# A four-layer graph network on one core: the Mamba block with chunks of 2, 2, 3, 4, 4, 4, 4, 3 tiles, the convolution in six paced steps per tile, taps and statistics one step later

## The chip, the core and the metric

The kernel runs on one core of a Trainium2 chip. It is one program, written in Python on the Tile framework, which traces the operations in program order, gives them priorities, orders them per engine and sets the semaphores. The engines are TensorE (PE: matmuls; its weight loads are PEld), VectorE (DVE), ScalarE (ACT), GpSimd (POOL) and SyncE (SP, which issues the DMAs). The metric is the device time of one execution in microseconds (us).

## What is computed

Four layers of a graph network on n = 3327 nodes with 256 features, all in float32. After each layer x becomes layernorm(x + layer(x, adj)). The change touches layer 1 alone, which is a graph convolution followed by a Mamba block:

```python
h = relu(adj @ x @ gcn_w + gcn_b)
h = layernorm(h) * ln_g + ln_b
xz = h @ w_in;  xc, z = xz[:, :512], xz[:, 512:]
u = silu(sum(xpad[k:k + L] * conv_w[:, k] for k in range(4)) + conv_b)
dbc = u @ w_xp
dt = softplus(dbc[:, :16] @ w_dt + b_dt)
B, C = dbc[:, 16:32], dbc[:, 32:]
dA = exp(dt[:, :, None] * -exp(A_log)[None])
h_t = dA_t * h_(t-1) + dt_t * B_t * u_t        # one scan along the nodes, for each of 512 channels x 16 states
y = (h_t @ C_t + u * D_skip) * silu(z)
out = y @ w_out
```

Layer 0 (a mean over neighbours), layer 2 (graph attention) and layer 3 (two steps of diffusion with a nucleus search) stand before and behind it. Layer 2 needs, for each row tile of layer 1's result, its product with a weight matrix and two attention columns; the program calls these the values and computes them in layer 1's stage.

## The kernel before

The 3327 nodes are 26 tiles of 128 rows (the last padded). In layer 1 three pieces of work run beside each other.

**The convolution** (`convolve`, lines 264 to 330) is a generator over the 26 tiles. For a tile it loads a column block of the adjacency matrix in three DMAs (line 275, 9 + 9 + 8 tiles of 128x128, `JC = 9`, two buffers), and sums 26 products into one PSUM bank `cb` (L276; each float32 matmul is two PE instructions in the profile). Then come a copy (L282), two transposes (L290), a copy (L292), the product with `gcn_w` (L294), the bias (L295) and relu (L297). What is left of the tile is put into a list `rest` that the next tile's loop works off: `measure` (bn_stats on VectorE, L84, then a power on GpSimd, L261, L262, L306), an empty step, `norm` (L309) and `turn` (transposes L318, two scaled copies into `hT`, L320). The generator yields four times for a tile: after j = 8 and 17, after the copy, and at the end. A tile counts as finished when it is turned, which is while the next tile is convolved; only the first tile does all its `rest` at once.

**The scan** goes through chunks of consecutive tiles, at most four (`WC = 512` columns). The chunks have 1, 2, 3, 4, 4, 4, 4, 4 tiles. For each chunk and each of 16 states, a "state" below, the main loop issues: two row loads from a DRAM scratch (L461), four scans on VectorE (L257, one for each group of 128 channels), their decays dA on ScalarE into two PSUM banks (L253), a copy of the last column (L566), the product with C (L257, 128x2048 at four tiles), the multiplication of dt u with B two states ahead on GpSimd (`feed`, L476), and transposes of the product that are summed in PSUM (`add_up`, L497, a bank for each tile of the chunk).

**The next chunk's inputs** are made by a generator `head(c + 1)`, one step in each of states 3 to 14 (lines 373 to 436): four projections (L369), each copied (L383) and multiplied by the first tap on ScalarE (L384), while VectorE adds three more taps to the group of the step before (L257, `u`); silu; `w_sp` (L398); the copy L401 and two DMAs to the scratch; two steps with two `w_dt` products each (L415, L417, L418); a step of exponentials and sums (L422, L423); then the logarithm and three operations of VectorE for `dt`; then `du` and the D-skip. Before state 3's step the main loop runs the convolution until all tiles of chunk c + 1 are finished. Beside that, each state of the main loop ends with one convolution step (`pump`, in the first chunk three of four states), and, when the convolution has ended, with one call of `values` instead (transposes L355, copy L357, product L360, two attention columns and an exponential L361 to L364). In states 0 to 5 gates (L502), residuals (L508, L510, L518, L519) and gate inputs (L445) of the old and the new chunk are added.

What orders this: each engine works off its queue in order. VectorE's scans, products, taps and dt operations are tied into one chain in program order (`chained`), ScalarE's decays and big activations into another (`decaying`); all else the framework places. One PSUM bank, `ps`, is shared by the projections, `w_sp`, `w_dt`, the turn, the gate inputs, the residuals and the values; each must be read out by ScalarE or VectorE before TensorE may write the next one.

The lines in which the pace is set:

```python
                ends.append(min(npad, prev + min(WC, (len(ends) + 1) * P)))
...
            pump(tiles=ends[0] // P)
            xs = {}
            for i, x in enumerate(head(0)):
                if i % 2:
                    pump()
...
                if DS - 13 <= s < DS - 1 and c + 1 < nch:
                    if s == DS - 13:
                        pump(steps=0, tiles=ends[c + 1] // P)
                        ahead = head(c + 1)
                    xs[c + 1] = next(ahead)
...
                if c or s % 4 < 3:
                    pump()
```

Of the kernel before, what the change touches and what calls it, by code (L numbers as in the profile page):

```python
# [9 lines left out]
F32 = mybir.dt.float32  # L10
BF16 = mybir.dt.bfloat16
I32 = mybir.dt.int32
AF = mybir.ActivationFunctionType
# [5 lines left out]
P = 128  # L19
# [3 lines left out]
J0 = 4  # L23
JC = 9
WC = 512
DI = 512
NG = DI // P
# [16 lines left out]
def gnn_kernel(ctx: ExitStack, tc: tile.TileContext, n: int, a: dict, out: bass.AP):  # L44
# [109 lines left out]
    with tc.tile_pool(name="l1b", bufs=1) as wpool, tc.tile_pool(name="l1at", bufs=2) as l1at:  # L154
# [33 lines left out]
        with tc.tile_pool(name="l1aw", bufs=1) as cwork, tc.tile_pool(name="l1c", bufs=2) as ch, \  # L188
# [54 lines left out]
            while not ends or ends[-1] < npad:  # L243
                prev = ends[-1] if ends else 0
                ends.append(min(npad, prev + min(WC, (len(ends) + 1) * P)))
            nch = len(ends)
# [17 lines left out]
            def convolve():  # L264
# [3 lines left out]
                for it in range(nt):  # L268
                    cb = cpsum.tile([P, 2, D], F32, name="cb")
                    acc, tp = cb[:, 0, :], cb[:, 1, :]  # L270
                    for j in range(nt):
                        if j % JC == 0:
                            m = min(JC, nt - j)
                            at = l1at.tile([P, JC, P], F32, name="at")
                            nc.sync.dma_start(at[:, :m, :], a["adjT"][it][:, j:j + m, :])
                        nc.tensor.matmul(acc, at[:, j % JC, :], X0[:, j, :], start=(j == 0), stop=(j == nt - 1))  # L276
                        if j % JC == JC - 1:
                            if rest:
                                rest.pop(0)()
                            yield full  # L280
                    m = cwork.tile([P, D], F32, name="m")
                    nc.scalar.copy(m, acc)  # L282
                    if rest:
                        rest.pop(0)()
                    yield full
                    if rest:
                        rest.pop(0)()
                        full += 1
                    for k in range(2):
# [21 lines left out]
                    def turn(it=it, h=h):  # L311
# [20 lines left out]
            stream = convolve()  # L332
            done = 0
            ready, valued = 0, 0

            def pump(steps=1, tiles=0):


                nonlocal done
                while steps > 0 or done < min(tiles, nt):  # L340
                    t = next(stream, None)
                    if t is None:
                        return values()
                    done, steps = t, steps - 1

            def values():

                nonlocal valued
                if valued == ready:
                    return  # L350
                it = valued
                valued += 1
# [11 lines left out]
                nc.scalar.mul(F[:, it, :D], po[:, :D], g)  # L364

            def project(c, g, w):
# [6 lines left out]
            def head(c):  # L373
# [6 lines left out]
                u = us[c] = ch.tile([P, NG, WC], F32, name="u", bufs=1)[:, :, :w]  # L380
                for g in range(NG + 1):
                    if g < NG:
                        nc.scalar.copy(xc[:, g, 3:3 + w], project(c, g, w))  # L383
                        nc.scalar.activation(u[:, g, :], xc[:, g, 0:w], AF.Identity, scale=conv_w[:, g, 0:1],  # L384
                                             bias=conv_b[:, g:g + 1])
                    if g:
                        ug = u[:, g - 1, :]
                        for k in range(1, 4):
                            chained(nc.vector.scalar_tensor_tensor, ug, xc[:, g - 1, k:k + w], conv_w[:, g - 1, k:k + 1], ug,
                                    op0=ALU.mult, op1=ALU.add)  # L390
                    if g < NG:
                        yield None
# [36 lines left out]
                dt = ch.tile([P, NG, WC], F32, name="dt", bufs=2)[:, :, :w]  # L429
                chained(nc.vector.scalar_tensor_tensor, dt, v, 0.0, e1, op0=ALU.max, op1=ALU.add)  # L430
                du = ch.tile([P, NG, WC], F32, name="du", bufs=1)[:, :, :w]
                yield None
                chained(nc.vector.tensor_mul, du, dt, u)
# [121 lines left out]
            for k, (c, s) in enumerate(states):  # L555
# [13 lines left out]
                if DS - 13 <= s < DS - 1 and c + 1 < nch:  # L569
                    if s == DS - 13:  # L570
                        pump(steps=0, tiles=ends[c + 1] // P)
                        ahead = head(c + 1)
                    xs[c + 1] = next(ahead)
# [32 lines left out]
            while valued < nt:  # L606
                values()


# [805 lines left out]
```

## Time and profile before

| | us |
|---|---|
| runs: median of three | 3623.58 |
| runs: lowest, highest | 3621.65, 3624.86 |
| the profiled execution | 3620.64 |
| its span, first to last instruction | 3618.6 |
| layer 1's stage in it: from layer 0's last aggregation matmul to layer 2's first | 354.0 to 1504.3 |
| first scan, last scan's end | 398.5, 1456.9 |

The span is 2.0 us shorter than the execution's own time, and that execution is 2.9 us faster than the median of the runs. In the page, "busy" is the time in which an engine had an instruction in work. In a window's row each engine has its busy time with the number of instructions in brackets, then the granted clock of TensorE as a share of full speed, the DMA share and the rate. A list of waits says which instruction stood idle for which other one, with the total, the number of times and the longest. In a timeline the columns are the start, the duration, the engine, the line, the operation, out<-in, shapes, how many were merged, and in brackets the idle time before it with what ended it. Lines of the Mamba block's chained operations are those of the helpers (L257 for VectorE, L253 for ScalarE); their tiles tell them apart: `h` is a scan, `hc` the product, `u` a tap, `dA` a decay, `t` and `dt` the softplus.

### The profile page before, as it was taken

How to read it: one execution, taken by the hardware profiler on the slowest of the kernel's cores; microseconds unless marked ns; L12 is line 12 of the kernel's file. 1: busy time of each engine (PE TensorE's matmuls, PEld its weight loads, DVE VectorE, ACT ScalarE, POOL GpSimd, SP SyncE). 2: the span in 40 equal slices, each digit the busy share in tenths (PEclk: the TensorE clock that was granted, in tenths of full speed). 3: DMA queues.
4: the chain of work that ended last, by engine and by line, in shares of the span. 5: the costliest groups of instructions: out<-in, count | busy, mean ns of one | idle time of the engine just before them, and what ended most of it. 6: DMA issues, size and time to landing. Idle time of an engine off the chain costs nothing. (4 is left out here: it accounts for less than half of the span.)

```text
span 3618.6 us, 43460 instructions
## 1 busy us (share of the span) xinstructions
PE 3287.3 (91%) x15583; PEld 2564.1 (71%) x15583; DVE 2414.3 (67%) x5460; ACT 1707.9 (47%) x2642; POOL 939.9 (26%) x970
## 2 busy tenths in 40 slices
PE   9999888888888765799979999999999899999996
PEld 7888666666666444588858777787786667777775
DVE  1111377889899888577753545445451999999996
ACT  1000465656656555211133333333335888888883
POOL 0000144556566545111110000000000233333332
PEclk9999999989998878799989999999999999999998
DMA  7443334334333122244422122121122122222210
GB/s 247 136 138 99 105 99 105 109 91 121 95 99 95 54 54 64 82 139 150 145 63 65 52 59 63 47 66 52 58 63 65 48 61 63 68 68 68 68 57 22
DMA packets 151997, 308.03 MB, mean 85 GB/s; under 512 B 19858, under 2 KB 73266, under 8 KB 151634
## 3 DMA queue, kind: packets, MB, share of 16 engines
q1 hardware_dynamic: 151762, 305.06, 28.1%
q8 instruction: 127, 2.08, 0.2%
q14 instruction: 108, 0.88, 0.1%
HBM read 294.36 MB, written 10.65 MB: 84 GB/s over the span
## 5 line engine op out<-in xcount | busy, mean ns | idle before, releaser
L476 POOL TENSOR_TENSOR h<-du,row 128x2048 f32<-128x2048 f32 (+3 forms) x128 | 475.3, 3714 | 432.9 <-DVE hc L257 301.9
L257 DVE TENSOR_TENSOR_SCAN h<-dA,carry,h 128x512 f32<-128x512 f32 (+2 forms) x448 | 496.8, 1153 | 47.2 <-ACT dA L253 46.9
L253 ACT ACTIVATE dA<-dt,A_log 128x512 f32<-128x512 f32 (+3 forms) x512 | 308.0, 609 | 241.4 <-DVE h L257 240.2
L858 PE MATMUL acc<-F,at 128*128 128x256 f32 x1352 | 352.5, 386 | 1.0 <-ACT q L632 0.6
L891 PE MATMUL acc<-X,wt 128*128 128x256 f32 x1352 | 343.6, 390 | 10.5 <-ACT wt L889 10.2
L891 PE MATMUL acc<-G,wt 128*128 128x256 f32 x1352 | 336.3, 392 | 5.9 <-ACT wt L822 5.3
L497 PE MATMUL y<-ident,hc 128*128 128x128 f32 x1664 | 256.3, 309 | 76.8 <-DVE hc L257 76.5
L276 PE MATMUL cb<-F,at 128*128 128x256 f32 x1352 | 320.9, 387 | 5.3 <-ACT hn L297 3.2
L497 PEld LDWEIGHTS y<-ident,hc 128*128 128x128 f32 x1664 | 224.5, 161 | 133.1 <-DVE hc L257 100.1
L891 PEld LDWEIGHTS acc<-X,wt 128*128 128x128 f32 x1352 | 242.5, 189 | 105.3 <-issue 41.3
L116 PE MATMUL acc<-xa,at 128*128 128x257 f32 x1352 | 309.1, 382 | 5.7 <-DMA at<-in_adjT 5.7
L858 PE MATMUL acc<-X,at 128*128 128x256 f32 x1352 | 308.4, 381 | 0.0
L767 PE MATMUL acc<-F,at 128*128 128x257 f32 x1352 | 303.9, 381 | 0.9 <-DMA U<-in_U 0.9
L276 PEld LDWEIGHTS cb<-F,at 128*128 128x128 f32 x1352 | 254.8, 194 | 59.1 <-issue 17.6
L891 PEld LDWEIGHTS acc<-G,wt 128*128 128x128 f32 x1352 | 250.1, 193 | 65.7 <-ACT wt L822 35.6
L903 DVE MAX8 cand<-e 128x8 f32<-128x128 f32 x676 | 142.3, 280 | 228.6 <-ACT e L844 217.1
L858 PEld LDWEIGHTS acc<-F,at 128*128 128x128 f32 x1352 | 237.1, 190 | 75.1 <-issue 50.2
L116 PEld LDWEIGHTS acc<-xa,at 128*128 128x128 f32 x1352 | 256.0, 191 | 42.7 <-issue 5.6
L858 PEld LDWEIGHTS acc<-X,at 128*128 128x128 f32 x1352 | 252.9, 191 | 39.8 <-issue 7.8
L767 PEld LDWEIGHTS acc<-F,at 128*128 128x128 f32 x1352 | 253.6, 191 | 36.6 <-issue 1.1
L257 DVE TENSOR_TENSOR hc<-h,row 128x2048 f32<-128x2048 f32 (+3 forms) x128 | 245.4, 1917 | 5.7 <-PE y L497 0.5
L889 ACT COPY wt<-tp 128x512 f32<-128x512 f32 (+1 forms) x182 | 93.7, 557 | 309.5 <-PE tp L887 308.9
(302 smaller groups left out, 5180.3 us busy)
## 6 DMA issues: line engine op xcount, KB each, us to landing
at<-in_adjT SPq DMA_DIRECT2D x102, 832.0 KB, 4.5
at<-in_adjT SPq DMA_DIRECT2D x260, 320.0 KB, 3.0
row<-bc SPq DMA_DIRECT2D x80, 512.0 KB, 4.8
at<-in_adjT SPq DMA_DIRECT2D x52, 576.0 KB, 4.3
at<-in_adjT SPq DMA_DIRECT2D x26, 512.0 KB, 3.8
row<-bc SPq DMA_DIRECT2D x16, 384.0 KB, 5.0
row<-bc SPq DMA_DIRECT2D x16, 256.0 KB, 4.8
xt<-in_xT SPq DMA_DIRECT2D x26, 128.0 KB, 4.1
```

The source lines that it names most:

```text
L116: nc.tensor.matmul(acc, at[:, j, :], rhs[:, j0 + j, :], start=(j0 + j == 0), stop=(j0 + j == nt - 1))
L253: decays.append(nc.scalar.activation(*x, **k))
L257: chain.append(op(*x, **k))
L276: nc.tensor.matmul(acc, at[:, j % JC, :], X0[:, j, :], start=(j == 0), stop=(j == nt - 1))
L476: nc.gpsimd.tensor_tensor(hs[k % 2][:, :, :w], du, rows[k][:, 0:1, :].to_broadcast([P, NG, w]), op=ALU.mult)
L497: nc.tensor.matmul(y[:, g * P:(g + 1) * P], h[:, g, i * P:(i + 1) * P], ident, is_transpose=True, start=(first and g == 0), stop=(last and ...
L767: nc.tensor.matmul(acc, at[:, j, :], F[:, j0 + j, :], start=(j0 + j == 0), stop=(j0 + j == nt - 1))
L858: nc.tensor.matmul(acc, at[:, j, :], rhs[:, j0 + j, :], start=(j0 + j == 0), stop=(j0 + j == nt - 1))
L889: copy(wt[:, :m, :], pt[:, :m, :])
L891: nc.tensor.matmul(acc, wt[:, j, :], rhs[:, j0 + j, :], start=(j0 + j == 0), stop=(j0 + j == nt - 1))
L903: nc.vector.max(cand[:, s * 8:(s + 1) * 8], z[:, s * SEG:(s + 1) * SEG])
```

## The change

The chunks become 2, 2, 3, 4, 4, 4, 4, 3 tiles. The convolution yields six times for a tile (after j = 5, 11, 17, 23, after the copy with all that is left of `rest`, and at the end), and `rest` begins with an empty step, so that the statistics come one step later. Instead of one step for each state, `pace` runs as many steps as keep the convolution even over the states, so that the tiles of chunk c + 1 are finished when state 3 of chunk c comes; in chunk 0's head it runs too. When the convolution has ended, `pace` makes two half values for each state: `value` yields between the copy of the transposed tile and the product. In `head` VectorE adds the taps of the group of two steps before, which takes one more step; the two `w_dt` steps issue their exponentials themselves, the second is issued in one step with the sums, and the early issue of the `w_dt` products is gone. The silu of the gate is issued in state 8 instead of 7.

```diff
-                ends.append(min(npad, prev + min(WC, (len(ends) + 1) * P)))
+                ends.append(min(npad, prev + min(WC, max(2, len(ends) + 1) * P)))
...
-                        if j % JC == JC - 1:
+                        if j % JM == JM - 1 and j < nt - 1:
                             if rest:
                                 rest.pop(0)()
                             yield full
                     m = cwork.tile([P, D], F32, name="m")
                     nc.scalar.copy(m, acc)
-                    if rest:
-                        rest.pop(0)()
+                    while rest:
+                        step = rest.pop(0)
+                        step()
+                        full += step is turn
                     yield full
-                    if rest:
-                        rest.pop(0)()
-                        full += 1
...
-                    rest = [measure, lambda: None, norm, turn]
+                    rest = [lambda: None, measure, lambda: None, norm, turn]
...
+            def advance():
+                nonlocal done, taken
+                t = next(stream, None)
+                if t is not None:
+                    done, taken = t, taken + 1
+                return t is not None
+
+            def pump(tiles):
+                while done < min(tiles, nt) and advance():
+                    pass
+
+            def pace(c, s):
+                c, s = divmod(c * DS + s + DS - 3, DS)
+                t0 = ends[c] if c < nch else npad
+                t1 = ends[c + 1] if c + 1 < nch else npad + P
+                target = NS * (t0 + (t1 - t0) * (s + 1) / DS) / P + NS - 1
+                while taken < target:
+                    if not advance():
+                        for _ in range(2):
+                            values()
+                        return
...
                 xt = cwork.tile([P, D], F32, name="m")
                 nc.scalar.copy(xt, pt[:, :D])
+                yield
                 po = psum.tile([P, WC], F32, name="ps")
...
+            def values():
+                nonlocal valued, valuing
+                if next(valuing, valuing) is None:
+                    return
+                if valued < ready:
+                    valuing = value(valued)
+                    valued += 1
+                    next(valuing)
...
-                for g in range(NG + 1):
+                for g in range(NG + 2):
...
-                    if g:
-                        ug = u[:, g - 1, :]
+                    if g > 1:
+                        ug = u[:, g - 2, :]
...
                 for g0 in range(0, NG, 2):
-                    pair = [psum.tile([P, WC], F32, name="ps") for _ in range(2)]
-
-                    with tc.high_priority():
-                        for g, ps in enumerate(pair, g0):
-                            k = slice(32 * g, 32 * g + DTR)
-                            nc.tensor.matmul(ps[:, :w], w_dt[k, :P], left[k], start=True, stop=True)
-                    for g, ps in enumerate(pair, g0):
+                    for g in range(g0, g0 + 2):
+                        ps = psum.tile([P, WC], F32, name="ps")
+                        k = slice(32 * g, 32 * g + DTR)
+                        nc.tensor.matmul(ps[:, :w], w_dt[k, :P], left[k], start=True, stop=True)
                         nc.scalar.activation(v[:, g, :], ps[:, :w], AF.Identity, bias=b_dt[:, g:g + 1])
                         nc.scalar.activation(e[:, g, :], ps[:, :w], AF.Abs, bias=b_dt[:, g:g + 1])
-                    yield None
+                        nc.scalar.activation(e[:, g, :], e[:, g, :], AF.Exp, scale=-1.0)
+                    if not g0:
+                        yield None
                 e1 = scratch()[:, :, :w]
                 for g in range(NG):
-                    nc.scalar.activation(e[:, g, :], e[:, g, :], AF.Exp, scale=-1.0)
                     nc.scalar.activation(e1[:, g, :], e[:, g, :], AF.Identity, bias=1.0)
...
-            pump(tiles=ends[0] // P)
+            pump(ends[0] // P)
             xs = {}
             for i, x in enumerate(head(0)):
-                if i % 2:
-                    pump()
+                pace(0, 3 - DS + i)
...
-                if s == 7:
+                if s == 8:
                     decaying(szs[c], szs[c], AF.Silu)
...
-                if c or s % 4 < 3:
-                    pump()
+                pace(c, s)
```

`JM` and `NS` are 6. `DS` is 16 states, `P` 128 rows, `nt` 26 tiles, `nch` 8 chunks.

More of the change, by code (lines that the diff above doesn't have):

```diff
@@ L24 @@
 JC = 9
+JM = 6
+NS = 6
 WC = 512
@@ L332, in gnn_kernel, with value @@
             stream = convolve()
[L333 to L352, printed above, removed]
+            done = taken = 0
+            ready, valued, valuing = 0, 0, iter(())
+            def advance():
[17 more added lines that the diff above has]
+                        return
+            def value(it):
                 pt = psum.tile([P, WC], F32, name="ps")
@@ L364, in values @@
                 nc.scalar.mul(F[:, it, :D], po[:, :D], g)
+                yield
+            def values():
[6 more added lines that the diff above has]
+                    next(valuing)
             def project(c, g, w):
@@ L385, in head @@
                                              bias=conv_b[:, g:g + 1])
-                    if g:
-                        ug = u[:, g - 1, :]
+                    if g > 1:
+                        ug = u[:, g - 2, :]
                         for k in range(1, 4):
-                            chained(nc.vector.scalar_tensor_tensor, ug, xc[:, g - 1, k:k + w], conv_w[:, g - 1, k:k + 1], ug,
-                                    op0=ALU.mult, op1=ALU.add)
-                    if g < NG:
+                            chained(nc.vector.scalar_tensor_tensor, ug, xc[:, g - 2, k:k + w], conv_w[:, g - 2, k:k + 1],
+                                    ug, op0=ALU.mult, op1=ALU.add)
+                    if g < NG + 1:
                         yield None
@@ L430, in head @@
                 chained(nc.vector.scalar_tensor_tensor, dt, v, 0.0, e1, op0=ALU.max, op1=ALU.add)
+                yield None
                 du = ch.tile([P, NG, WC], F32, name="du", bufs=1)[:, :, :w]
-                yield None
                 chained(nc.vector.tensor_mul, du, dt, u)
@@ L566, in gnn_kernel @@
                     nc.scalar.copy(carry[:, s, :], hs[k % 2][:, :, w - 1])
-                if s == 7:
+                if s == 8:
                     decaying(szs[c], szs[c], AF.Silu)
-                if DS - 13 <= s < DS - 1 and c + 1 < nch:
-                    if s == DS - 13:
-                        pump(steps=0, tiles=ends[c + 1] // P)
+                if 3 <= s < DS - 1 and c + 1 < nch:
+                    if s == 3:
+                        pump(ends[c + 1] // P)
                         ahead = head(c + 1)
@@ L607, in gnn_kernel @@
                 values()
+            values()
     half = nt // 2 * P
```

## The prediction

> **What bounds the kernel now.** The page's first and second parts came first: the change lies in one stage, the Mamba block, and the shares of the whole span say little about it.
>
> ```profile
> span 3618.6 us, 43460 instructions
> ...
> PE 3287.3 (91%) x15583; PEld 2564.1 (71%) x15583; DVE 2414.3 (67%) x5460; ACT 1707.9 (47%) x2642; POOL 939.9 (26%) x970
> ```
>
> The page's chain that ended last names only the final store, so the stage was cut by hand into windows at the first scan of each chunk (found in the timeline: 398.5, 487.3, 589.0, 722.6, 874.5, 1023.5, 1172.0, 1330.3, last scan done 1456.9). First row: start-up before any scan; then the eight chunks of 1, 2, 3, 4, 4, 4, 4, 4 tiles; last row: the tail up to layer 2.
>
> ```profile
> core 0: us, PE busy (x) PEld busy (x) DVE busy (x) ACT busy (x) POOL busy (x), PEclk, DMA share, GB/s
> 354.00:398.00 44.00, 40.57 (x193) 31.85 (x192) 10.37 (x28) 19.82 (x47) 3.93 (x9) 1.00 0.29 92
> 398.00:487.00 89.00, 77.05 (x334) 57.76 (x334) 48.27 (x104) 51.67 (x143) 27.57 (x30) 0.92 0.35 100
> 487.00:589.00 102.00, 92.01 (x430) 68.83 (x429) 80.36 (x109) 65.14 (x145) 46.41 (x34) 0.95 0.43 112
> 589.00:722.00 133.00, 115.55 (x516) 84.29 (x515) 108.60 (x114) 77.88 (x147) 66.66 (x37) 0.90 0.39 102
> 722.00:874.00 152.00, 133.27 (x635) 100.01 (x633) 136.17 (x117) 86.89 (x150) 87.76 (x34) 0.92 0.37 107
> 874.00:1023.00 149.00, 127.65 (x616) 95.67 (x616) 136.77 (x121) 87.96 (x152) 88.67 (x35) 0.93 0.36 104
> 1023.00:1172.00 149.00, 118.72 (x576) 88.80 (x576) 137.46 (x121) 87.85 (x152) 89.13 (x35) 0.91 0.31 89
> 1172.00:1330.00 158.00, 110.12 (x448) 72.96 (x448) 135.18 (x113) 93.63 (x183) 76.88 (x23) 0.78 0.21 54
> 1330.00:1457.00 127.00, 78.77 (x390) 61.04 (x390) 115.79 (x97) 64.16 (x129) 71.44 (x19) 0.83 0.22 58
> 1457.00:1504.00 47.00, 32.78 (x117) 23.02 (x117) 14.52 (x42) 13.58 (x35) 4.22 (x12) 0.67 0.14 54
> ```
>
> The third busy column is DVE. In the eight chunks it sums to 898.6 us of 1059, so VectorE with its scans is the bound, with 160.4 us idle: 40.7, 21.6, 24.4, 15.8, 12.2, 11.5, 22.8, 11.2 by chunk. TensorE is busy 87 to 90% in chunks 1 to 3, so there it is nearly the bound too. The start-up holds 10 us of DVE work in 44. Next, what DVE waited for in this stage (354 to 1504):
>
> ```profile
> engine line waited for: us in total, times, longest us
> DVE h L257 <- ACT dA L253: 59.5, 50, 5.7
> DVE bnst L84 <- ACT hn L297: 57.8, 11, 17.3
> DVE u L257 <- ACT u L384: 51.8, 27, 5.2
> DVE X L519 <- PE ps L518: 16.6, 4, 7.2
> ```
>
> The second line is statistics of a convolved tile standing in DVE's queue ahead of scans, the third the convolution taps doing so: both block scans behind them until ScalarE delivers. The fourth is the tail.
>
> **1. Start-up.** With a first chunk of two tiles the program waits for two finished tiles, and a tile is finished (turned) only in the next tile's last part, so three tiles are convolved before the first projection, where one was. Rows of the timeline:
>
> ```profile
> 367.74 0.44 PE L290 MATMUL cb<-ident,m 128*128 128x128 f32 x2 [0.51 <-ACT m L282]
> ...
> 370.92 2.00 PE L276 MATMUL cb<-F,at 128*128 128x256 f32 x8 [0.47 <-ACT hn L297]
> ...
> 375.15 0.61 PE L369 MATMUL ps<-hT,w_in 128*128 128x128 f32 x4
> ...
> 417.81 11.41 PE L276 MATMUL cb<-F,at 128*128 128x256 f32 x52
> ```
>
> A dense convolution is 11.4 us, its tail (from 367.2 to the next tile's start at 370.9) 3.7. So: 370.9 + 11.4 + 0.4 (the turn) + 3.7 + 11.4 = 397.9; the turn of tile 1 and its two ScalarE copies (0.4 + 0.4 + 2 x 0.4, as at 373.6 to 375.15) put the first projection at about 400, 25 later than 375.15. The head of chunk 0 then took 23.4 us (375.15 to 398.5) at one tile. At two tiles, in the built program's order, 24 pairs of convolution matmuls (0.44 us each) lie between its first projection and w_sp where 13 did (+4.8), four projections take 1.03 instead of about 0.65 (+1.5), and a gcn and bias piece of 1.8 with half a us of waiting for its accumulator stands among them: +9. The w_dt part: +2 (ScalarE rows of 256 instead of 128 columns). The DVE chain of four (0.69 each at one tile, half of the 2.3 at four tiles, 1.15, at two), and the first feed, 2.35 for 1.27: +3. First scan at about 437.5, **+39 us**. A second count agrees: before the first product's transposes TensorE now has 5.0 tiles of convolution where it had 2.7, 2.3 x 15.1 = 35 us. Bounds 30 and 46.
>
> **2. DVE work.** The tiles are the same 26 and the instructions as many; only widths move. Scans (rows 409, 734, 999, 1267 ns for 1 to 4 tiles): 2 x 0.734 + 2 x 0.999 + 4 x 1.267 against 0.409 + 0.734 + 0.999 + 5 x 1.267, times 64: +3.6. Products (831, 1304, 1755, 2289 ns, times 16): -1.0; taps (351, 565, 619, 752, times 12): +1.0. **+3.6 us.**
>
> **3. Idle time in the chunks.** Chunk 0 of one tile goes: its 40.7 idle us were the forced convolution (19.0 for statistics, one wait of 17.3; 12.6 for dA). Taps come a step later: the data they read were issued a whole state earlier, so their 46.6 us inside chunks (51.8 less 5.2 in the start-up) should go; what is late next is dA, whose waits I keep. Statistics come a sixth of a tile later: their waits shrink to 0 to 2. Merging the second w_dt pair with the exponentials puts 6 x 0.65 + 4 x 0.62 + the state's 4 x 0.69 = 9.1 us on ScalarE in one state of 7.1 DVE us; the old layout had up to 7.8. ScalarE is 57 to 59% busy in the four-tile windows and the scheduler spreads it, so 0, with 2 a chunk if that cover fails. TensorE, counted from the built order at full clock, gets 62, 86, 103, 108 and 112 us in chunks 0 to 4, where the old order had 83, 100, 115 and 113 in chunks 1 to 4: so c1 and c2 stay near TensorE's bound and I leave 5 us each for it. Convolution still ends in chunk 5, so the last two chunks hold the same value work, in two steps: the tap waits of c6 go (5.5), its 6.4 for e1 and 10.0 for dA stay; c7 has ten values instead of nine beside states of 5.3 us instead of 7.1, I take 12. Idle by chunk after: c0 11 (21.6 of the old two-tile chunk, less 7.9 for taps and 2.8 of its 4.8 for statistics), c1 16 (that and 5), c2 16 (24.4 - 9.4 - 4 + 5), c3 10 (15.8 - 8.2 + 2 for TensorE), c4 6 (12.2 - 6.2), c5 6 (11.5 - 5.1), c6 17, c7 12, in all 94: **-66 us**. Bounds: 60 (dA waits shrink too) and 141 (every width idles as now: 21.6 + 21.6 + 24.4 + 15.8 + 12.2 + 11.5 + 22.8 + 11.2).
>
> **4. Tail.** Three last tiles instead of four, three values instead of four. The timeline gives residuals 3.8 to 5.6 apart (1462.4, 1466.2; 1482.6 to 1488.2) and 4.2 per value (1488.7 to 1492.9): **-9 us**; bounds -6 and -12.
>
> **At nothing.** The adjacency loads keep size and number (78), and so do the row loads; on SP's queue a row load may stand behind an adjacency load that waits for its buffer, but all matmuls waited 2.1 us for such loads in this stage, and POOL's multiplications have 2.6 us of slack per four-tile state (7.1 less 4.5). The table loads are as many in both built programs. The D-skip and du edits move an allocation, no instruction. If POOL's cover failed it would be 1 us in some states.
>
> [...] The granted clock was 0.90 to 0.95 in the chunks with convolution and 0.78 and 0.83 in the last two without. [...] By the rows it is 0.9 still, since total work per chunk stays. I take the rows.
>
> **Sum.** 39 + 3.6 - 66 - 9 = -32 us. The profiled execution took 3620.6 (span 3618.6 and 2 around it): 3588. The median of the runs is 2.9 above that execution: **3591**.
>
> **Rivals.**
> (a) The waits change their name: taps no longer wait for u, but scans behind them wait for dA or the product's transposes as long. For it: ScalarE's queue is in order, dA is already the largest wait (59.5), and c1 to c3 have TensorE near 90%. Against it: the tap waits are short (1 to 2 us) and sit in states whose dA came in time. Then idle is 141 and the sum 39 + 3.6 - 19 - 9 = +14, **3638, slower**. The point that decides: idle in the chunks above 127 us.
> (b) TensorE takes over in c1 to c4 only: 7 more us each than forecast: 3591 + 28, **3619**, within 0.2%.
> (c) The dA waits shrink as well, since fewer bunches stand ahead of them, and the start-up comes at its lower bound: idle 60, first scan +31: 39 - 8 + 3.6 - 100 - 9 = -74, **3549**.
> (d) The scheduler undoes the pacing: its built order was read, and taps and statistics do stand a state later, so this is only a small chance, and falls under (b).
>
> **Chances and range.** Forecast 0.60 (3570 to 3608), (a) 0.14, (b) and (d) 0.14, (c) 0.12. The range leaves out most of (a) and half of (c): 3560 to 3622. A measurement here can tell about 0.2% from no change, 7 us. Faster by more than that: the forecast, (c) and a third of (b), 0.77; within: most of (b) and an edge of (a), 0.11; slower: 0.12.
>
> **What would show it.** Right: first scan at 432 to 443; no wait of u on ACT u in the chunks above 1 us; idle between 85 and 105; four-tile chunks of 141 to 146 us before convolution ends; tail near 38. Wrong: first scan beyond 446, or dA waits above 80 us in the stage, or a granted clock near 0.8 in chunks 1 to 5.

## The result, and the profile after

The changed kernel takes 3631.39 us (median of 20 runs, 3622.35 to 3638.18) against 3621.19 before (20 runs): the ratio is 1.0025, 95% interval 1.0017 to 1.0034. It is a quarter of a per cent slower, where 3591 us, about 0.9% faster, was forecast.

The page of the profiled execution (3631.3 us):

```profile
span 3629.5 us, 43459 instructions
...
PE 3275.3 (90%) x15583; PEld 2562.6 (71%) x15583; DVE 2412.7 (66%) x5460; ACT 1709.0 (47%) x2642; POOL 937.9 (26%) x967
```

The same work in 11 us more. The windows, cut again at the first scan of each chunk; first row the start-up, last row the tail:

```profile
core 0: us, PE busy (x) PEld busy (x) DVE busy (x) ACT busy (x) POOL busy (x), PEclk, DMA share, GB/s
354.00:442.00 88.00, 82.33 (x333) 64.70 (x332) 15.07 (x31) 28.77 (x60) 7.92 (x15) 0.90 0.32 95
442.00:526.00 84.00, 69.86 (x332) 52.98 (x331) 72.08 (x102) 57.85 (x136) 44.30 (x26) 0.92 0.38 100
526.00:630.00 104.00, 92.30 (x448) 70.72 (x446) 80.50 (x111) 66.24 (x146) 48.23 (x34) 0.97 0.42 110
630.00:766.00 136.00, 115.86 (x539) 85.32 (x538) 111.00 (x114) 78.34 (x147) 68.40 (x35) 0.94 0.38 103
766.00:918.00 152.00, 126.03 (x592) 91.93 (x592) 134.71 (x116) 86.83 (x150) 86.20 (x34) 0.91 0.35 101
918.00:1075.00 157.00, 126.51 (x616) 95.29 (x616) 136.87 (x122) 88.35 (x152) 86.48 (x34) 0.91 0.35 98
1075.00:1224.00 149.00, 107.10 (x522) 79.55 (x522) 136.62 (x122) 85.96 (x146) 86.76 (x34) 0.89 0.29 80
1224.00:1371.00 147.00, 99.47 (x448) 70.87 (x448) 131.17 (x113) 89.70 (x183) 76.13 (x21) 0.84 0.22 56
1371.00:1471.00 100.00, 67.02 (x328) 51.40 (x328) 90.32 (x95) 56.42 (x131) 54.27 (x19) 0.84 0.28 56
1471.00:1510.00 39.00, 25.00 (x95) 18.00 (x95) 12.72 (x39) 11.06 (x29) 3.20 (x9) 0.70 0.17 62
```

The start-up holds 88 us instead of 44, as meant. The tail is 39 instead of 47. The second chunk has two tiles as before and lasts 104 us where it took 102, with the same 80.5 us of VectorE. The four-tile chunk at 918 takes 157 us where the one at 874 took 149, with the same 136.9 us of VectorE (136.8 before). What VectorE waited for in the stage (354 to 1510):

```profile
engine line waited for: us in total, times, longest us
DVE bnst L86 <- ACT hn L298: 64.3, 9, 16.5
DVE h L259 <- ACT dA L255: 55.9, 43, 4.2
DVE t L259 <- ACT t L445: 46.6, 7, 12.4
DVE u L259 <- ACT u L408: 23.8, 6, 16.1
```

The taps (`u`) fell from 51.8 to 23.8, and of these 20.7 lie in the start-up: inside the chunks they wait 3.1 us instead of 46.6, as forecast. But `t`, the first operation of the softplus, now stands third with 46.6 us of waiting for the sums on ScalarE. Before, the same table had it far down:

```profile
DVE t L257 <- ACT t L423: 7.0, 2, 6.4
```

Inside the chunks the taps lost 43.5 us of waiting and t gained 33.4 (6.4 to 39.8): most of the time that left one line came back under another.

How it comes about, in the four-tile chunk at 918. First the kernel before, the timeline of the w_dt series that makes t:

```profile
965.76 1.12 PE L415 MATMUL ps<-t,w_dt 16*128 16x512 f32 x2 [0.21 <-ACT t L401]
...
987.18 0.63 ACT L423 ACTIVATE t<-t 128x512 f32<-128x512 f32 x1
...
990.20 2.27 DVE L257 SCALAR_TENSOR_TENSOR t<-t 128x2048 f32<-128x2048 f32 x1
```

From the first product to the last sum are 22 us, about three states of 7.1; VectorE comes to t at 990.2, 2.4 us after the series has ended, and does not wait. The same series in the changed kernel:

```profile
1019.73 1.12 PE L437 MATMUL ps<-t,w_dt 16*128 16x512 f32 x2
...
1025.72 0.69 ACT L255 ACTIVATE dA<-dt,A_log 128x512 f32<-128x512 f32 x1 [2.73 <-DVE h L259]
1026.34 0.67 ACT L438 ACTIVATE t<-ps,b_dt 128x512 f32<-128x512 f32 x1
...
1027.64 2.07 PE L437 MATMUL ps<-t,w_dt 16*128 16x512 f32 x2 [5.01 <-ACT t L439]
...
1032.47 0.63 PE L319 MATMUL ps<-ident,hn 128*128 128x128 f32 x2
...
1034.37 1.12 PE L437 MATMUL ps<-t,w_dt 16*128 16x512 f32 x2
...
1036.85 1.12 PE L437 MATMUL ps<-t,w_dt 16*128 16x512 f32 x2 [0.88 <-ACT t L439]
...
1040.20 1.66 ACT L445 ACTIVATE t<-t 128x512 f32<-128x512 f32 x3
...
1041.89 2.29 DVE L259 SCALAR_TENSOR_TENSOR t<-t 128x2048 f32<-128x2048 f32 x1 [12.41 <-ACT t L445]
...
1046.52 4.53 POOL L498 TENSOR_TENSOR h<-du,row 128x2048 f32<-128x2048 f32 x1 [17.40 <-DVE hc L259]
```

Each product writes the one bank `ps`, and the next may start only when ScalarE has read it twice; ScalarE's queue has the decays ahead of that reading (the one at 1025.72 itself waited 2.73 us for a scan), and a turn (L319) takes the bank in between. From 1019.7 to 1041.9 are again 22 us. ScalarE is not the limit by its load: in the window 1019 to 1042 it is busy 15.8 of 23 us. But t now stands in VectorE's queue 9.8 us after the first product, so it waits 12.4, and the product, the scans and GpSimd (17.4 us idle) stand behind it.

Measured so in every trace (**series**: first w_dt product's start to the last sum's end; **room**: that start to the moment VectorE comes to t), for the heads that prepare chunks 3 to 6 (four tiles in both kernels):

| kernel | series, us | room, us |
|---|---|---|
| before | 16.3, 21.7, 22.0, 21.7 | 19.2, 24.1, 24.4, 24.1 |
| changed | 18.8, 17.6, 22.1, 17.5 | 15.3, 7.6, 9.8, 19.8 |

The series is about as long as before; what the change took away is the room. In the head for chunk 3 even 10.6 of the 15.3 us are a wait: the statistics of a convolved tile stand in VectorE's queue just ahead of t.

### The profile page after: what moved, and what is told of

Same layout as the page of the kernel before. It is cut to its first block, busy times and chain, and to the rows that moved or that the text cites. A ratio compares the mean times of both kernels' runs of the same rounds, so it can differ in the third digit from the quotient of the medians.

```text
span 3629.5 us, 43459 instructions
## 1 busy us (share of the span) xinstructions
PE 3275.3 (90%) x15583; PEld 2562.6 (71%) x15583; DVE 2412.7 (66%) x5460; ACT 1709.0 (47%) x2642; POOL 937.9 (26%) x967
## 3 DMA queue, kind: packets, MB, share of 16 engines
HBM read 294.36 MB, written 10.65 MB: 84 GB/s over the span
## 5 line engine op out<-in xcount | busy, mean ns | idle before, releaser
L498 POOL TENSOR_TENSOR h<-du,row 128x2048 f32<-128x2048 f32 (+2 forms) x128 | 475.6, 3716 | 411.4 <-DVE hc L259 310.3
L259 DVE TENSOR_TENSOR_SCAN h<-dA,carry,h 128x512 f32<-128x512 f32 (+2 forms) x448 | 478.8, 1113 | 54.3 <-ACT dA L255 51.3
L255 ACT ACTIVATE dA<-dt,A_log 128x512 f32<-128x512 f32 (+2 forms) x512 | 309.0, 609 | 232.0 <-DVE h L259 228.0
L912 PE MATMUL acc<-X,wt 128*128 128x256 f32 x1352 | 345.2, 392 | 10.5 <-ACT wt L910 10.2
L278 PE MATMUL cb<-F,at 128*128 128x256 f32 x1352 | 333.6, 397 | 12.2 <-ACT hn L298 12.1
L278 PEld LDWEIGHTS cb<-F,at 128*128 128x128 f32 x1352 | 263.6, 200 | 69.2 <-ACT hn L298 18.2
L519 PEld LDWEIGHTS y<-ident,hc 128*128 128x128 f32 x1664 | 217.2, 157 | 130.9 <-DVE hc L259 100.0
L879 PEld LDWEIGHTS acc<-X,at 128*128 128x128 f32 x1352 | 252.9, 191 | 39.8 <-issue 6.6
L259 DVE TENSOR_TENSOR hc<-h,row 128x2048 f32<-128x2048 f32 (+2 forms) x128 | 246.5, 1926 | 4.7
```

What stands on the lines that cost most here:

```text
L255: decays.append(nc.scalar.activation(*x, **k))
L259: chain.append(op(*x, **k))
L498: nc.gpsimd.tensor_tensor(hs[k % 2][:, :, :w], du, rows[k][:, 0:1, :].to_broadcast([P, NG, w]), op=ALU.mult)
L519: nc.tensor.matmul(y[:, g * P:(g + 1) * P], h[:, g, i * P:(i + 1) * P], ident, is_transpose=True, start=(first and g == 0), stop=(last and ...
L879: nc.tensor.matmul(acc, at[:, j, :], rhs[:, j0 + j, :], start=(j0 + j == 0), stop=(j0 + j == nt - 1))
L912: nc.tensor.matmul(acc, wt[:, j, :], rhs[:, j0 + j, :], start=(j0 + j == 0), stop=(j0 + j == nt - 1))
```

## The experiments

Theory: the merged step gives t too little room, and this wait cancels what the later taps save. Rivals: the pacing, the chunks or the dropped early issue cost the time. The kernel before was run beside each set and came to 3620.5 to 3621.4 us, so the medians can be compared across sets. Ratios to before have intervals of about 0.0009 to 0.0013 on either side, 3 to 5 us. Each trace is one execution and can lie some us from its run's median: e5's took 3603.2 us, e10's 3589.2, e16's 3602.7.

**e1 and e2: the head step alone, undone or done.** e1 is the changed kernel with before's `head`; e2 is before with the changed `head`. The edit, to and fro:

```diff
-                    if g > 1:
-                        ug = u[:, g - 2, :]
+                    if g:
+                        ug = u[:, g - 1, :]
...
+                    pair = [psum.tile([P, WC], F32, name="ps") for _ in range(2)]
+                    with tc.high_priority():
...
-                        nc.scalar.activation(e[:, g, :], e[:, g, :], AF.Exp, scale=-1.0)
-                    if not g0:
-                        yield None
+                    yield None
                 e1 = scratch()[:, :, :w]
                 for g in range(NG):
+                    nc.scalar.activation(e[:, g, :], e[:, g, :], AF.Exp, scale=-1.0)
```

> The changed kernel with the whole head step of before (w_dt products in two steps and issued early, exponentials in a third, taps one group after their projection); chunks, pacing and values stay changed. Theory (the merged w_dt and exponential step makes a new wait that cancels what the taps saved): the wait of DVE's t for ScalarE falls from 46.6 us to under 12, the taps' wait for u inside the chunks returns from 3.1 us to 25 to 47, and the time stays within 0.3% of the changed kernel, 3622 to 3641 us. Rival 1 (the head's edits are a gain of some 40 us that the pacing or the chunks eat): 3660 us or more. Rival 2 (the head's edits are a pure loss): 3605 us or less.

Measured: 3624.46 us, ratio 1.0008 (0.9999 to 1.0017). t's wait is 7.0, the taps' is 42.6 inside the chunks.

> The kernel before with the changed head step alone. Theory (the merged step makes its wait wherever it stands): taps' waits for u inside the chunks fall from 46.6 us to under 5, the wait of t for ScalarE rises from 7.0 to 35 to 50, and the time is within 0.3% of before, 3610 to 3632 us. Rival (the wait at t needs the new pacing, which puts a turn and a convolution tail beside it): t waits under 15 us and the time is 3580 to 3595 us.

Measured: 3618.44 us, ratio 0.9993 (0.9984 to 1.0003). The waits inside its chunks (399 to 1450):

```profile
DVE t L257 <- ACT t L421: 44.6, 7, 9.4
...
DVE u L257 <- ACT u L384: 8.9, 4, 4.8
```

Both times and t's wait are as the theory has it (the taps in e2 keep 8.9 us, not under 5): the head's edits exchange one wait of some 45 us for another, with the old pacing too. They are worth -3 us in the old kernel, which is within its interval, and +7 in the new.

**e3 and e4: the chunks alone**, undone in the changed kernel (e3) and done in before (e4):

```diff
-                ends.append(min(npad, prev + min(WC, (len(ends) + 1) * P)))
+                ends.append(min(npad, prev + min(WC, max(2, len(ends) + 1) * P)))
```

> The changed kernel with the old chunks of 1, 2, 3, 4, 4, 4, 4, 4 tiles. Theory that the two-tile first chunk does not repay its start-up: first scan near 400 us instead of 442.2, and the time is 10 to 25 us below the changed kernel, 3606 to 3621. Rival (the chunks are worth what was predicted, 28.7 us gone with the first chunk's idle time against 39, with the tail 9 and the rest of a shorter idle, so about even or a gain): 3631 to 3650 us.

Measured: 3640.49 us, ratio 1.0058 (1.0045 to 1.0071); first scan at 413.8.

> The kernel before with the chunks of 2, 2, 3, 4, 4, 4, 4, 3 tiles alone. Theory that the start-up is not repaid: 39 to 44 us later at the first scan, some 25 to 35 less in the chunks, 8 less in the tail: 3621 to 3635 us. Rival (the one-tile chunk's idle 40.7 us goes whole, and with it 20 more): 3600 us or less.

Measured: 3615.98 us, ratio 0.9989 (0.9977 to 1.0001); first scan at 438.4, last scan's end 1457.3, as before. The time lies between the two forecasts. The theory that the start-up is not repaid failed in e3: the new chunks are worth 9 us in the changed kernel and perhaps 5 in the old one. They are not the cause of the loss.

**e5: the merged step split again.** The head gets 13 steps and starts at state 2:

```diff
                         nc.scalar.activation(e[:, g, :], e[:, g, :], AF.Exp, scale=-1.0)
-                    if not g0:
-                        yield None
+                    yield None
...
-                if 3 <= s < DS - 1 and c + 1 < nch:
-                    if s == 3:
+                if 2 <= s < DS - 1 and c + 1 < nch:
+                    if s == 2:
...
-                c, s = divmod(c * DS + s + DS - 3, DS)
+                c, s = divmod(c * DS + s + DS - 2, DS)
```

> The changed kernel with the merged step split again: the second pair of w_dt products with its exponentials in one step, the sums e1 in the next; so the head has 13 steps and starts at state 2 of the chunk before, and the pacing aims a state earlier. Taps stay two steps behind their projection. Theory (what a single state must do for w_dt, exponentials and sums is the new wait): t's wait for ScalarE falls from 46.6 us to under 12, the taps' stay under 10 inside the chunks, and the time falls by 30 to 40, to 3591 to 3602 us. Rival (ScalarE and the single product bank are late there however the steps are cut, so the wait moves to another instruction): under 10 us gained, 3621 us or more.

Measured: 3595.14 us, ratio 0.9924 (0.9911 to 0.9937), 36 us below the changed kernel. t's wait inside the chunks is 6.6 us, the taps' 4.9; room 16.4, 21.5, 22.7, 25.0. The theory holds in sign and size; in the whole stage t still waits 13.4 us, as 6.8 in the start-up stay. dA's wait rose from 55.9 to 77.8, so part of it did change its name.

**e6: the early issue back**, the merged step kept:

```diff
+                    pair = [psum.tile([P, WC], F32, name="ps") for _ in range(2)]
+                    with tc.high_priority():
+                        for g, ps in enumerate(pair, g0):
```

> The changed kernel with the w_dt products of a pair issued early again, as before; the merged step stays. If the dropped early issue made the wait: t's wait for ScalarE falls from 46.6 to under 20 us and the time to 3600 to 3612. If the amount of work in the one state made it: t's wait stays above 35 us and the time within 0.3% of the changed kernel, 3622 to 3641 us.

Measured: 3634.88 us, ratio 1.0034 (1.0021 to 1.0047); t's wait 54.7. The dropped early issue is not the cause.

**e7 and e8: the old pacing.** e7 is the changed kernel with before's `convolve` and `pump`; e8 is that with e5's split.

```diff
-                        if j % JM == JM - 1 and j < nt - 1:
+                        if j % JC == JC - 1:
...
-                    rest = [lambda: None, measure, lambda: None, norm, turn]
+                    rest = [measure, lambda: None, norm, turn]
...
-                pace(c, s)
+                if c or s % 4 < 3:
+                    pump()
```

> The changed kernel with the convolution's old pacing (a step every nine tiles, one step per state, the turn and the statistics where they were); chunks, head step and two-step values stay changed. Theory from the four runs before (chunks alone 5 us below the kernel before, head alone 3 below, so the pacing costs what is left): about 18 us below the changed kernel, 3606 to 3620. Rival (each part only loses beside the others): 3625 us or more.

Measured: 3655.33 us, ratio 1.0089 (1.0076 to 1.0102); t's wait 63.2. The rival's range, not the theory's.

> The run above with the merged step split as in the first of these runs: new chunks, taps two steps behind, old pacing, 13 steps from state 2. If both reasons hold and add up: t's wait under 12 us, the taps' under 10, time 3570 to 3590, below both kernels. If the waits only change their names: 3605 us or more.

Measured: 3612.70 us, ratio 0.9974 (0.9963 to 0.9985); t's wait 24.2, the taps' 16.0: again the rival's range. The sum that I made from the first four runs failed: the parts do not add up, and the pacing gains 24 us beside the merged step and 18 beside the split one. The split is worth 43 us here.

**e9 and e10: where t is queued.** e9 splits the step but keeps 12 steps from state 3 (the last two groups of taps share a step with the silu of u). e10 keeps the merged step as it is, puts an empty step behind it and starts at state 2. First e9's edit, then e10's:

```diff
-                    if g < NG + 1:
+                    if g < NG:
                         yield None
...
-                    if not g0:
-                        yield None
+                    yield None
```

```diff
                     nc.scalar.activation(e1[:, g, :], e[:, g, :], AF.Identity, bias=1.0)
                 yield None
+                yield None
                 chained(nc.vector.scalar_tensor_tensor, e, e1, 1.0, e, op0=ALU.subtract, op1=ALU.subtract)
```

> The changed kernel with the merged step split, but still 12 steps from state 3: the last two groups of taps share a step with the Silu of u instead, so that neither the head's start nor the pacing moves. Theory (the merge of the w_dt work was the fault): t's wait for ScalarE under 15 us instead of 46.6 and 3592 to 3608 us. Rival (the 36 us that the split gained came from starting the head and the convolution a state earlier): 3622 us or more.

Measured: 3605.20 us, ratio 0.9961 (0.9948 to 0.9974); t's wait 10.2, the taps' 37.7 with the start-up. So 26 us of the 36 come without an earlier head. For the other 10 the taps that now stand in one state are the likely bearer (17.3 us in the chunks, 4.9 in e5), but e5's earlier start is not told apart from it.

> The changed kernel with the merged step kept as it is and an empty step behind it, so that t is queued a state later; 13 steps from state 2, with the pacing a state earlier. If t only stood too early in VectorE's queue for what the merged step asks of ScalarE: its wait falls under 12 us, the dA wait stays under 85, and the time is within 7 us of the split version's 3595, 3588 to 3602. If the crowd of ten activations in one state holds up the other things that ScalarE owes: dA's wait rises over 90 us and the time is 3610 us or more.

Measured: 3593.93 us, ratio 0.9925 (0.9913 to 0.9936). Its waits inside the chunks (440 to 1432):

```profile
DVE h L259 <- ACT dA L255: 66.0, 48, 3.2
...
DVE t L259 <- ACT t L445: 6.6, 2, 4.3
```

The ten activations stand in one state as in the changed kernel, the series lasts 17.5, 18.7, 19.2, 17.0, and with the room at 13.3, 20.7, 21.3, 27.6 the loss is gone. So it isn't the crowd on ScalarE: t was queued a state too early. (In the stage t still waits 13.5 us, 6.8 of it in the start-up.)

**e11 and e12: the old chunks with the split, and the taps alone.** e11 is e5 with the old chunks (e3's edit). e12 is the kernel before with taps two steps behind, its three w_dt steps and the early issue kept, 13 steps from state 2:

```diff
-                for g in range(NG + 1):
+                for g in range(NG + 2):
...
-                    if g:
-                        ug = u[:, g - 1, :]
+                    if g > 1:
+                        ug = u[:, g - 2, :]
...
-                if DS - 13 <= s < DS - 1 and c + 1 < nch:
-                    if s == DS - 13:
+                if DS - 14 <= s < DS - 1 and c + 1 < nch:
+                    if s == DS - 14:
```

> The split version of 3595 us (13 steps from state 2) with the old chunks of 1, 2, 3, 4, 4, 4, 4, 4. Theory from the changed kernel, where the old chunks cost 9.1 us: 3600 to 3610 us, with the first scan near 413 and the tail at 47. Rival (with the wait at t gone the late start weighs more than the short last chunk saves): 3590 us or less.

Measured: 3597.83 us, ratio 0.9945 (0.9932 to 0.9957). This lies between the two forecasts: the chunks are worth 2.7 us here, within the intervals.

> The kernel before with nothing changed but the taps, which come two steps behind their projection instead of one; the w_dt work stays in three steps, issued early, so the head has 13 steps and starts at state 2. Theory of the prediction (the taps' 46.6 us of waits go, and nothing behind them is late): 3575 to 3592 us. Rival (with the convolution's old pacing the waits change their name, as the old-paced split version with its 3613 us against 3616 for the chunks alone suggests): u's wait under 10 us inside the chunks but dA's, t's and the statistics' together 25 or more above the 124.3 of before, and 3610 to 3622 us.

Measured: 3592.23 us, ratio 0.9929 (0.9916 to 0.9941). This one edit, at the edge of its theory's range, gives nearly all the gain that was forecast for the whole change (28 us against 32). Its waits inside the chunks (399 to 1428):

```profile
DVE h L257 <- ACT dA L253: 69.6, 47, 4.5
DVE u L257 <- ACT u L384: 17.2, 10, 2.9
```

The taps keep 17 of 46.6 us, dA gains 10, the product now waits 7.7 for its sums' transposes, the statistics lose half (35.4 to 16.6): VectorE's idle time in the chunks falls by 29 us (159.8 to 131.1). The rival with its change of names was wrong by the time, though part of the waits did move.

**e13 to e16: chunks, pacing and step form beside e12's head.** e13 is e12 with the new chunks, e14 with chunks and pacing, e15 with the pacing alone. e16 is e12 with e10's head (merged, not issued early, t a state later). The edits are those above.

> The version of 3592 us (before, taps two steps behind) with the new chunks of 2, 2, 3, 4, 4, 4, 4, 3, old pacing. If the chunks are worth what they were worth beside the old taps (5 us): 3582 to 3592 us. Rival (the late start is not repaid when the waits that a shorter chunk plan also removed are gone): 3600 to 3618 us.

> The same with new chunks, the new pacing and two-step values: the changed kernel with taps two steps behind, and the w_dt work left in its three steps, 13 steps from state 2. If the new pacing gains with the new chunks as it did for the split version (18 us): 3565 to 3590 us. Rival (the pacing only helps where products aren't issued early): 3590 to 3605 us, as the split version's 3595.

> The same with the old chunks and the new pacing. If chunks and pacing are independent: the 3592 us of the old pacing less the 18 of the pacing, about 3575. Rival (the new pacing only repairs what the new chunks upset, as 3598 for the split version with old chunks suggests): 3588 to 3603 us.

> The kernel before with taps two steps behind and the w_dt work merged as in the change, without early issue, but t a state after it: old chunks, old pacing, 13 steps. If merging costs nothing once t stands a state later: within 7 us of 3592, 3585 to 3599. Rival (the early issue or the three steps matter with the old pacing): 3603 us or more, with t's wait above 30 us.

Measured, all heads side by side (medians, us):

| chunks, pacing | taps and w_dt as before | changed head | merged, t later | split, not early | three steps, early |
|---|---|---|---|---|---|
| old, old | 3621 | 3618 (e2) | 3610 (e16) | | 3592 (e12) |
| new, old | 3616 (e4) | 3655 (e7) | | 3613 (e8) | 3600 (e13) |
| old, new | | 3640 (e3) | | 3598 (e11) | 3608 (e15) |
| new, new | 3624 (e1) | 3631 (changed) | 3594 (e10) | 3595 (e5) | 3600 (e14) |

The ratios are 0.9945 (0.9932 to 0.9959) for e13, 0.9945 (0.9931 to 0.9958) for e14, 0.9966 (0.9952 to 0.9979) for e15, 0.9969 (0.9959 to 0.9979) for e16. e13 and e14 fell into their rivals' ranges, e15 into neither (above both). In each row the changed head is slower than the heads to its right, by 8 to 55 us.

The pacing goes with the chunks: with the old ones it loses 22 and 16 us (e2 to e3, e12 to e15); with the new ones it gains 24 and 18 beside the changed and the split head (e7 to the changed kernel, e8 to e5), nothing beside e12's (e13 to e14), and loses 8 beside the old head (e4 to e1). What is called pacing here is not quite one edit: the two-step values and the later silu of the gate come with it, but stay in e7 and e8, and no run sets them alone.

e16's rival was right: with the old pacing and no early issue the room is 15.5, 15.5, 17.9, 19.2 even a state later, and t waits 33.1 us in the stage. In e13 against e12 the first scan is 43.3 us later, the chunks take 1000.0 instead of 1028.4, the tail 36.4 instead of 48.2: the late start is just about repaid in the stage (+3 at layer 2's start; the medians differ by 8, of which 5 lie behind layer 1 in these traces).

What stays open: why the pacing's worth runs from -22 to +24 us with its company; these runs show that it does, not by which wait. No version found beats e12, e10 and e5, whose 3592 to 3595 the runs do not tell apart.

## Why the prediction was wrong, point by point

| step | forecast, us | measured, us |
|---|---|---|
| start-up, first scan | +39 (30 to 46) | +43.6 (398.5 to 442.2) |
| VectorE's work in the chunks | +3.6 | -4.8 (898.6 to 893.8) |
| idle in the chunks | -66 (160.4 to 94) | -24.2 (159.8 to 135.6, cut at the scans themselves) |
| tail | -9 | -8.3 (47.4 to 39.1) |
| sum | -32 | +6.3 (layer 2 starts at 1510.6, before 1504.3) |

The rest of the 11 us of span lies behind layer 1, in code that the change does not touch: 2118.9 us from layer 2's first matmul to the end, 2114.2 before. Over the traces of all these kernels this part takes 2112 to 2123 us, without a pattern that I could find.

**The step that failed** is in the third part: "Merging the second w_dt pair with the exponentials puts [...] 9.1 us on ScalarE in one state of 7.1 DVE us [...] so 0, with 2 a chunk if that cover fails." I weighed the load of an engine where a series of dependent steps decided. The series had 22 us in the profile of before and the reader t stood just 24 us behind its start; both could be read from the timeline rows above. The change leaves it 8 to 20 us of room. Priced at nothing, this costs 36 to 37 us by e10 and e5, whose heads also start a state earlier, and 26 by e9, whose head does not; by the waits of t, 33 inside the chunks (6.4 to 39.8). With the room given back the forecast's idle by chunk comes out near what was written:

| chunk | 0 | 1 | 2 | 3 | 4 | 5 | 6 | 7 | sum |
|---|---|---|---|---|---|---|---|---|---|
| forecast | 11 | 16 | 16 | 10 | 6 | 6 | 17 | 12 | 94 |
| changed | 11.8 | 23.5 | 25.0 | 17.3 | 20.1 | 12.4 | 15.8 | 9.7 | 135.6 |
| e10 | 12.4 | 16.8 | 13.9 | 10.5 | 10.2 | 10.8 | 15.0 | 8.9 | 98.5 |

e10's sum at layer 2's start is 1470.7 - 1504.3 = -33.6 us; the forecast was -32. That these agree so well is partly luck: this execution is 4.7 us below e10's median, which is 27 us below before, and in it dA (66.0) and the statistics (11.5) wait longer than forecast while VectorE works less. In e5's trace the idle sums to 109.1.

**The taps** did what was said: their waits in the chunks went from 46.6 to 3.1 us. "What is late next is dA, whose waits I keep" holds for the total (59.5 to 55.9), but it was not next; t was. **The statistics** went from 35.4 inside the chunks to 25.6, not to 0 to 2. Most of it is the failed step under another name. In two heads they stand just ahead of t while the series runs; the rows of the first:

```profile
606.05 0.43 DVE L86 BATCH_NORM_STATS2 bnst<-hn 128x6 f32<-128x256 f32 x1 [8.51 <-ACT hn L298]
...
609.14 1.76 DVE L259 SCALAR_TENSOR_TENSOR t<-t 128x1536 f32<-128x1536 f32 x1 [2.45 <-ACT t L445]
```

In the second the two waits are 10.65 and 3.49 us. In e6 the statistics come behind t in both heads and do not wait there, and t waits 10.94 and 10.25. So 19 of the 25.6 us lie in the same standstill, which ends with the series in either order; in e6 the statistics wait 4.3 in the chunks, in e5 and e10 7.2 and 11.5.

**The start-up** was mis-sized by 4.6. The first projection came at 402.2 for "about 400": the third tile's 52 products took 13.3 us instead of 11.4, at a granted clock of 0.88 (387 to 401) where the start-up of before had 1.00. Then the head took 40.0 us (402.2 to 442.2) for a forecast of 37.5; in it t waits 6.8 us (0.6 before). That is not the merged step: e5 and e10 keep these 6.8 us, and e1, with the old head, has 7.0; e4, the new chunks alone, has 0.5. Which edit makes it the runs do not settle.

**VectorE's work**: the scans were to cost 3.6 us more; they sum to 542.6 before and 541.6 after. I had priced chunk 0's scans of 256 columns at the 0.734 us of the later ones, which read a carry; without a carry they took 0.675, which makes 3.8 us over 64 of them. The head of chunk 0, now of two tiles, also moves work out of the chunks into the start-up, which I had left out: in the chunks the taps take 57.2 for 59.3 and the softplus operations with du 55.3 for 57.3.

**The clock**: the prediction took the rows of before and left it at 0.9. With runs of six tiles chunks 0 to 5 were granted 0.92, 0.97, 0.94, 0.91, 0.91, 0.89, before 0.92, 0.95, 0.90, 0.92, 0.93, 0.91. The rows of before proved right; that it is because the work per chunk stays was my argument and is not shown by a run. Of the prediction's signs of being wrong none came: first scan 442.2 (beyond 446), dA 55.9 (above 80), clock 0.89 to 0.97 (near 0.8).

**The rivals**: (a), waits that change their name with idle above 127 us, is what came (135.6; 3638 forecast, 3631 measured), but with another bearer: it named dA and the transposes, and the wait was for the merged step. It had 0.14. The decision point was right, and the trace of before could have told which wait would take the place.

## What to carry to other kernels

When steps of a pipeline are merged or moved, measure in the trace how long the whole series of dependent instructions lasts, from its first producer to the reader, and compare it with the distance at which the reader is queued; a busy share under 60% (here ScalarE's 57 to 59% in chunks 3 to 6 of the kernel before) said nothing about that. The products that went through one PSUM bank here paid the reader's queue on ScalarE as well (7.9 us from one product's start to the next with decays ahead, 2.5 without), and what else uses the bank (a turn, at 1032.47) stood in between. A reader queued one state too early blocked an in-order engine and cost 26 to 37 us; with a state more in e10 the same work cost next to nothing. It is the room that counts, not the step added: in e16, with the old pacing, the same empty step left a room of 15.5 to 19.2 us, and t still waited 33.1 us.

## What the runs showed of the hardware

The w_dt products follow each other at 2.5 us (1034.37 and 1036.85) when ScalarE is free to read the bank, and at 7.9 us (1019.73 and 1027.64) when decays stand ahead in its queue. What a second bank would gain is not shown, as no run here gave these products one; the stage's others are four for the sums, two for the decays and `cb`.

The granted clock fell to 0.88 in the start-up while TensorE was busy 13.5 of 14 us (387 to 401); in the start-up of before, with 40.6 of 44 us (354 to 398), it was 1.00. The mean hides one short stretch: between 388 and 392 the granted clock was 0.57, and in the windows on either side (384 to 388, 392 to 402) 1.00. The stretch follows the end of a tile, in which TensorE was busy 2.55 of 4 us (384 to 388). In the start-up of before TensorE was busy 3.01 of 4 us at the end of a tile (368 to 372) without a fall of the clock. What lowers it is not shown.
